# A two-layer hybrid network on one Trainium2 core: causal masks on the later keys alone, and a reciprocal in four pieces

## The chip, the cores and the metric

The kernel runs on one core of one Trainium2 chip. A core has a matrix engine (TensorE, PE in the profile, with its weight loads as PEld), a vector engine (VectorE, DVE), an engine for activations (ScalarE, ACT), a general one (GpSimd, POOL), and queues that issue DMAs (SyncE, SP, and others). Each engine works through its own instructions in order, and they wait for one another by semaphores. [...]

The metric is the device time of one execution in microseconds (us).

## The reference

The input is a batch of 32 sequences of 256 tokens with 128 features. Eight blocks are added to it one after the other, each behind a layer norm: a two-way state-space block, a mixture of experts, a recurrence, the same mixture again, then a windowed attention, a sparse mixture of experts, a causal attention with rotary positions, and a second sparse mixture. The change touches the two attentions. What they have in common, and where they differ:

```python
# the causal attention (the second one): 16 heads of 8 features
scores = jnp.einsum('bhqd,bhkd->bhqk', Q, K) / jnp.sqrt(jnp.float32(D_K))
causal = jnp.tril(jnp.ones((s, s), dtype=bool))
scores = jnp.where(causal[None, None], scores, -jnp.inf)
attn = jax.nn.softmax(scores, axis=-1)
out = jnp.einsum('bhqk,bhkd->bhqd', attn, V)

# the windowed attention (the first one): a query sees the up to 128 keys before it
allowed = (dist > 0) & (dist <= w) & (k_gpos[:, None, :] >= 0)
```

The softmax needs a maximum over each query's allowed keys, the exponentials, and a division by their sum.

## The kernel before

The features lie on the 128 partitions, and the tokens along the free dimension, in 16 chunks of 512 tokens (two sequences). A stage runs over the chunks as a software pipeline: `pipeline(chunk, 16, newest=True)` starts a chunk every 16 steps of the one before, so that two to three chunks are interleaved, and the order of the instructions on each engine follows from where the generators yield. The stages are the state-space block (up to about 2300 us in the profile), the first layer's mixtures and recurrence, the first attention (`l1_attn_a`, about 3370 to 4480 us) with the routing of its sparse mixture (`send`), the experts' blocks, the second attention (`l1_attn_b`, about 4970 to 6020 us) with the collection of what came before (`fetch`) and another routing, and again the experts' blocks.

Both attentions call `attend`. Its first pass only finds the maxima. For each of the two sequences (b), a first group of four PSUM banks takes the scores of the first 128 queries; then, for each half x of the heads, four banks take those of the last 128 queries against all 256 keys (two heads side by side in a bank, `j`, each with 256 keys, `k`). In each bank a bf16 matmul of an identity with a mask table writes 0 or -1e30 (`add_mask`, L918, which opens the accumulation), and a matmul of queries and keys adds the scores (L955 for the first queries, L978 for the second). VectorE takes the maximum over the keys (L964 and L982). The banks come from one pool with five buffers (tag `st`).

The second pass transposes the maxima, folds them into the queries (L1001 to L1004), and computes scores with the keys on the partitions: later keys with later queries (L1020), earlier keys with all queries (L1038). They go into banks of the same pool. ScalarE takes the exponential (L1029 and L1042), GpSimd sets the disallowed ones to zero (L922), and PE weighs the values with them (`weigh`, L1056), the sums of the exponentials coming along as a ninth row of each head. At the end of a chunk the sums are spread over the features of their heads (`dps`, L1093), VectorE takes the reciprocal of that 128x512 bank (L1095), the weighed values are packed (`ops`, L1099), and their product (L1100) is the attention's result. The output projection follows (L1643 in the second attention).

`masks.second` is what the mask matmul of the last 128 queries writes. For the windowed attention it lets a query at position q + 128 see the keys from q on to q + 127, and for the causal one (`k <= q1`) those up to q + 128. In the causal case every key of the first 128 is allowed.

Of the kernel before, what the change touches and what calls it, by code (L numbers as in the profile page):

```python
# [22 lines left out]
P = 128  # L23
B, L = 32, 256
# [170 lines left out]
def shape_constants():  # L195

    c = Packed()
    c.add("ident", np.eye(P, dtype=np.float32))
    c.add("center", np.eye(P, dtype=np.float32) - np.float32(1.0 / P))
    c.add("mean", np.full((P, 1), 1.0 / P, np.float32))  # L200
    c.add("mhalf", np.full((P, 8), -0.5, np.float32))
    c.add("states", (np.arange(P)[:, None] // 4 == np.arange(32)[None]).astype(np.float32))
    c1 = Packed()
    c1.add("rev", np.tile(np.arange(E, 0, -1, dtype=np.float32), (P, 4)))
    feat = np.arange(P)

    par = (feat[:, None] // 16) % 2 == np.arange(2)[None]
    c1.add("par", par.astype(np.float32))
    c1.add("ninth", (feat[:, None] % 16 == HD).astype(np.float32))
    for x in range(2):  # L210
        pk, dn = np.zeros((2, 8, 16, H, HD), np.float32)
        for h in range(8):
            pk[h, :HD, 8 * x + h, :] = np.eye(HD)
            dn[h, HD, 8 * x + h, :] = 1.0
        c1.add(f"pack{x}", pk.reshape(P, P))
        c1.add(f"den{x}", dn.reshape(P, P))
    c1.add("earlier", (np.arange(P)[:, None] < np.arange(P)[None]).astype(np.float32))
    c1.add("ones", np.ones((P, P), np.float32))
    c1.add("region", np.tile(np.arange(E, dtype=np.float32) * ROWS, (P, 1)))
    c1.add("filled", np.arange(0, NT, BLK, dtype=np.float32)[None])  # L220
    c1.add("upto", (np.arange(E)[None] <= np.arange(E)[:, None]).astype(np.float32).reshape(1, -1))
    c1.add("block", np.arange(NBLK, dtype=np.float32)[None])


    tok = np.arange(P)[:, None, None] + P * np.arange(4)[None, :, None]
    c1.add("home", (1.0 + 2 * tok + np.arange(2)[None, None]).reshape(P, 8))
    row = np.arange(P)[:, None, None] + BLK * np.arange(NBLK)[None, :, None] + P * np.arange(BLK // P)[None, None]
    c1.add("nowhere", (1.0 + 2 * NT + row).reshape(P, NBLK * BLK // P))
    c1.add("lheads", (np.arange(32)[:, None] // HD == np.arange(LH)[None]).astype(np.float32))

    rv = np.zeros((P, 2, 32), np.float32)
    for pr in range(2):
        for j in range(2):
            h = 2 * pr + j
            rv[j * NLAT : (j + 1) * NLAT, pr, h * HD : (h + 1) * HD] = 1.0
    c1.add("rvmask", rv)
    half = HD // 2
    inv = np.float32(10000.0) ** (-np.arange(half, dtype=np.float32) * np.float32(2.0) / np.float32(HD))
    ang = (np.arange(L, dtype=np.float32)[:, None] * inv[None]).astype(np.float32)
    at = (feat % HD) // 2  # L240
    used = (feat % 16 < HD)[:, None]
    cos = np.cos(ang)[:, at].T * used
    sin = np.sin(ang)[:, at].T * np.where(feat % 2 == 0, -1.0, 1.0)[:, None] * used
    c1.add("cosq", cos * SCALE)
    c1.add("sinq", sin * SCALE)
    c1.add("cosk", cos)
    c1.add("sink", sin)

    q = np.arange(P)[:, None]
    k = np.arange(L)[None]  # L250

    def add_mask(allowed, reps):
        return np.tile(np.where(allowed, 0.0, NEG), (1, reps))

    q1 = q + P
    first = (k < q)[:, :P]
    window = (k < q1) & (k >= q1 - P) & (k >= 1)
    lat = np.arange(NLAT)[None]
    masks = np.concatenate(
        [  # L260
            np.eye(P),
            add_mask(first, 4),
            add_mask(window, 2),
            add_mask((k <= q)[:, :P], 4),
            add_mask(lat < q // 4, LH),
            add_mask(lat < q1 // 4, LH),
            add_mask(k <= q1, 2),
        ],
        axis=1,
    ).astype(ml_dtypes.bfloat16)  # L270
    return c, c1, masks
# [3 lines left out]
def hybrid_kernel(ctx: ExitStack, tc, x_d, out_d, d, packs):  # L275
    nc = tc.nc
# [365 lines left out]
    mask_t = late.tile([P, d["masks"].shape[1]], BF16, name="mask_t")  # L642
# [271 lines left out]
    def rows(r):  # L914
        return slice(32 * r, 32 * r + 32)

    def add_mask(o, m):
        nc.tensor.matmul(o, identb, m, start=True, stop=False, skip_group_check=True)  # L918
# [14 lines left out]
    def attend(pools, qT, kT, kb, values, nms, masks, out):  # L933
# [5 lines left out]
        m_q0, m_q1 = masks.first, masks.second  # L939

        def banks():
            return [ps.tile([P, CH], F32, tag="st", name="st", bufs=5) for r in range(T)]
# [3 lines left out]
        for b in range(2):  # L946
            q0, q1 = slice(b * L, b * L + P), slice(b * L + P, (b + 1) * L)
            cut = slice(b * L, (b + 1) * L)
            n0, n1 = (t.rearrange("p (x h f) -> p x h f", x=2, h=8)[:, :, :, HD] for t in nms[b])
            s0 = banks()  # L950
            for o in s0:
                add_mask(o, m_q0)
            for x in range(2):
                for r, o in enumerate(s0):
                    nc.tensor.matmul(  # L955
                        o[:, x * L : (x + 1) * L],
                        qT[x][rows(r), q0],
                        kb[x][rows(r), :, q0],
                        start=False,
                        stop=True,  # L960
                        skip_group_check=True,
                    )
            for r, o in enumerate(s0):
                nc.vector.tensor_reduce(  # L964
                    n0[:, :, 2 * r : 2 * r + 2],
                    o.rearrange("p (x j k) -> p x j k", x=2, j=2),
                    AX.X,
                    ALU.max,
                    negate=True,
                )  # L970
            yield
            yield
            for x in range(2):
                s1 = banks()
                for o in s1:
                    add_mask(o, m_q1)
                for r, o in enumerate(s1):
                    nc.tensor.matmul(  # L978
                        o, qT[x][rows(r), q1], kb[x][rows(r), :, cut], start=False, stop=True, skip_group_check=True
                    )  # L980
                for r, o in enumerate(s1):
                    nc.vector.tensor_reduce(  # L982
                        n1[:, x, 2 * r : 2 * r + 2],
                        o.rearrange("p (j k) -> p j k", j=2),
                        AX.X,
                        ALU.max,
                        negate=True,
                    )
                yield
                yield  # L990
            if masks.window:

                nc.gpsimd.memset(nms[b][0][0:1, :], 0.0)
# [97 lines left out]
        dps = ps.tile([P, CH], F32, tag="m", name="dps")  # L1091
        for x in range(2):
            nc.tensor.matmul(dps, K(f"den{x}"), avs[x], start=(x == 0), stop=(x == 1))  # L1093
        rden = p2.tile([P, CH], F32, tag="rden", name="rden", bufs=1)
        nc.vector.reciprocal(rden, dps)  # L1095
        yield
        ops = ps.tile([P, CH], F32, tag="m", name="ops")
        for x in range(2):
# [39 lines left out]
    mo = P  # L1138
    m_first, m_window, m_causal, m_lat = (mask_t[:, mo + n * 512 : mo + (n + 1) * 512] for n in range(4))
    masks_a = Masks(m_first, m_window, True, 0)  # L1140
    masks_b = Masks(m_causal, mask_t[:, mo + 4 * 512 : mo + 5 * 512], False, 1)

# [275 lines left out]
    def l1_attn_a(send):  # L1420
        with ExitStack() as ph:
# [117 lines left out]
            def chunk(c):  # L1539
# [27 lines left out]
                for k, _ in enumerate(attend((p2, p3, ps), qT, kT, kb, values, nms, masks_a, local)):  # L1567
                    if k > 15:
                        next(side, None)
                    yield  # L1570
# [30 lines left out]
    def l1_attn_b(fetch, send):  # L1601
        with ExitStack() as ph:
# [6 lines left out]
            def chunk(c):  # L1609
# [25 lines left out]
                def values(b):  # L1635
                    project_values(ps, xin[:, b * L : (b + 1) * L], W("Wv"), None, vbs[b])
                    return vbs[b]

                yield from attend(
                    (p2, p3, ps), *([rot[n, y] for y in range(2)] for n in "qk"), kb, values, nms, masks_b, o  # L1640
                )
# [54 lines left out]
```

## Time and profile before

| | |
|---|---|
| median of 3 runs | 6514.0 us (6503.61 to 6520.93) |
| the profiled execution's own time | 6514.91 us |
| its span, first to last instruction | 6513.1 us |
| granted TensorE clock, mean over the span | 0.885 |
| TensorE busy | 5594.1 us (86%) |
| VectorE busy | 4202.2 us (65%) |
| ScalarE busy | 2688.5 us (41%) |
| GpSimd busy | 3325.7 us (51%) |
| mask matmuls (L918) | 768, of 0.379 us each in the median |
| reciprocals of the denominators (L1095) | 32, of 3.358 us each |

A busy share is a mean over stages with different limits. In a row of the timeline the first number is the start in us, the second the length of a run of like instructions (the last number behind x says how many), and a bracket gives how long the engine stood idle before it and what ended that. Successive matmuls overlap, so the pace of a run is the distance of its starts and not the length of one. The granted clock is the share of full speed at which TensorE ran.

### The profile page before, as it was taken

How to read it: one execution, taken by the hardware profiler on the slowest of the kernel's cores; microseconds unless marked ns; L12 is line 12 of the kernel's file. 1: busy time of each engine (PE TensorE's matmuls, PEld its weight loads, DVE VectorE, ACT ScalarE, POOL GpSimd, SP SyncE). 2: the span in 40 equal slices, each digit the busy share in tenths (PEclk: the TensorE clock that was granted, in tenths of full speed). 3: DMA queues.
4: the chain of work that ended last, by engine and by line, in shares of the span. 5: the costliest groups of instructions: out<-in, count | busy, mean ns of one | idle time of the engine just before them, and what ended most of it. 6: DMA issues, size and time to landing. Idle time of an engine off the chain costs nothing. (4 is left out here: it accounts for less than half of the span.)

```text
span 6513.1 us, 73037 instructions
## 1 busy us (share of the span) xinstructions
PE 5594.1 (86%) x25538; PEld 2738.9 (42%) x25538; DVE 4202.2 (65%) x6974; ACT 2688.5 (41%) x4391; POOL 3325.7 (51%) x3074
## 2 busy tenths in 40 slices
PE   6777777777777789999999899897998999998897
PEld 2111111111111146686544444443885444444786
DVE  5888888888888855304555555554665666664565
ACT  4555555555555435434433434433221332333221
POOL 4777777777777746304544444443332333333232
PEclk8888888888888789859999999997998999998898
DMA  3223223223223283000000000001552000000555
GB/s 149 110 92 123 104 91 118 110 95 120 104 92 119 77 331 138 1 1 1 1 1 4 9 9 8 10 9 45 188 188 67 14 17 17 17 14 11 168 186 189
DMA packets 190416, 512.20 MB, mean 79 GB/s; under 512 B 22176, under 2 KB 75168, under 8 KB 164960
## 3 DMA queue, kind: packets, MB, share of 16 engines
q1 hardware_dynamic: 172192, 468.14, 20.0%
q0 software_dynamic: 17280, 35.69, 1.6%
q8 instruction: 202, 3.31, 0.2%
q10 hardware_dynamic: 576, 3.71, 0.1%
q14 instruction: 166, 1.36, 0.1%
HBM read 360.06 MB, written 147.38 MB: 78 GB/s over the span
## 5 line engine op out<-in xcount | busy, mean ns | idle before, releaser
L598 POOL TENSOR_TENSOR dBu<-widedu,bcB 128x512 f32<-128x512 f32 x1024 | 1326.4, 1310 | 464.2 <-DVE h L607 340.3
L561 PE MATMUL yps<-pr,cst_t 128*32 128x512 f32 x2048 | 936.9, 731 | 492.2 <-DVE pr L609 214.7
L607 DVE TENSOR_TENSOR_SCAN h<-dA,dBu 128x512 f32<-128x512 f32 x768 | 941.1, 1225 | 68.9 <-POOL dBu L598 12.3
L922 POOL TENSOR_SCALAR_AFFINE_SELECT e<-e 128x2048 f32<-128x2048 f32 (+1 forms) x256 | 342.5, 1350 | 617.0 <-ACT e L1029 397.6
L561 PEld LDWEIGHTS yps<-pr,cst_t 128*32 128x32 f32 x2048 | 116.1, 117 | 1201.8 <-DVE pr L609 406.1
L594 ACT ACTIVATE dA<-widedelta,Af 128x510 f32<-128x510 f32 x512 | 348.9, 688 | 563.0 <-DVE h L607 440.4
L1392 POOL DMA_INDIRECT rows_out<-y,goes x284 | 271.8, 957 | 559.1 <-DVE y L1390 481.7
L982 DVE TENSOR_REDUCE nm<-st 128x2 f32<-128x512 f32 x512 | 324.1, 684 | 291.5 <-PE st L978 291.5
L594 ACT ACTIVATE dA<-widedelta,Ab 128x510 f32<-128x510 f32 x512 | 347.4, 687 | 394.5 <-DVE h L607 294.2
L1167 ACT ACTIVATE s<-s 128x512 f32<-128x512 f32 x284 | 178.9, 630 | 577.0 <-DVE s L1166 347.2
L315 POOL TENSOR_TENSOR rstd<-var,cst_t 128x4 f32<-128x4 f32 x128 | 130.0, 1015 | 521.5 <-DVE var L313 519.8
L767 POOL TENSOR_TENSOR comb<-comb,ye 128x512 f32<-128x512 f32 x224 | 284.8, 1275 | 181.8 <-DVE ye L766 75.2
L607 DVE TENSOR_TENSOR_SCAN hs<-dA,dBu 128x512 f32<-128x512 f32 x256 | 310.6, 1213 | 95.4 <-POOL dBu L598 95.4
L1042 ACT ACTIVATE e<-st 128x512 f32<-128x512 f32 x512 | 271.7, 598 | 175.3 <-PE st L1038 174.4
L556 POOL TENSOR_TENSOR pr<-hs,bcC 128x512 f32<-128x512 f32 x256 | 338.5, 1322 | 1.4 <-DVE hs L607 1.4
L609 DVE TENSOR_TENSOR pr<-h,bcC 128x1024 f32<-128x1024 f32 x256 | 309.8, 1210 | 8.0 <-PE yps L561 0.9
L1281 POOL DMA_INDIRECT rows_in<-xt,slot x256 | 254.0, 992 | 119.4 <-issue 99.4
L1373 PE MATMUL g_ps<-xb,gu 128*128 128x256 f32 x1136 | 302.6, 389 | 3.6 <-ACT xb L1356 2.3
L1168 DVE TENSOR_TENSOR hh<-s,u_ps 128x512 f32<-128x512 f32 x284 | 195.4, 688 | 170.2 <-ACT s L1167 164.2
L1382 PE MATMUL yps<-dn,hh 128*128 128x128 f32 x2272 | 291.0, 275 | 5.1 <-DVE hh L1168 5.1
L1373 PE MATMUL u_ps<-xb,gu 128*128 128x256 f32 x1136 | 293.3, 381 | 0.0
L1382 PEld LDWEIGHTS yps<-dn,hh 128*128 128x128 f32 x2272 | 282.6, 192 | 14.1 <-DVE hh L1168 6.6
(348 smaller groups left out, 11083.1 us busy)
## 6 DMA issues: line engine op xcount, KB each, us to landing
gu<-in_gu SPq DMA_DIRECT2D x142, 512.0 KB, 3.8
rows_in<-zero SPq DMA_DIRECT2D x60, 1170.0 KB, 18.8
widedelta<-delta_d SPq DMA_DIRECT2D x64, 1024.0 KB, 6.8
widedu<-du_d SPq DMA_DIRECT2D x64, 1024.0 KB, 5.0
dn<-in_dn SPq DMA_DIRECT2D x142, 256.0 KB, 4.0
bcB<-xdbl_d SPq DMA_DIRECT2D x32, 1024.0 KB, 7.6
bcC<-xdbl_d SPq DMA_DIRECT2D x32, 1024.0 KB, 7.3
xr<-rows_in SPq DMA_DIRECT2D x142, 130.0 KB, 3.9
```

What stands on the lines that cost most here:

```text
L556: nc.gpsimd.tensor_mul(pr, hs, bc["C"][:, g, :])
L561: nc.tensor.matmul(yps[32 * k : 32 * k + 32, :], K("states"), pr, start=False, stop=(g == 3), skip_group_check=True, tile_position=(0, 32 ...
L594: nc.scalar.activation(two(dA)[:, :, 1:L], two(steps)[:, :, 1:L], AF.Exp, scale=A[s][:, at : at + 1])
L598: nc.gpsimd.tensor_mul(dBu, duw[:, k, :], bc["B"][:, g, :])
L607: nc.vector.tensor_tensor_scan(*views, 0.0, ALU.mult, ALU.add)
L609: nc.vector.tensor_mul(pr2, h2, bc["C"][:, g, :].unsqueeze(1).to_broadcast([P, 2, CH]))
L767: nc.gpsimd.tensor_add(comb, comb, ye)
L922: nc.gpsimd.affine_select(e, e, [[0, n], [sign, P]], ALU.is_gt, 0.0, base=base, channel_multiplier=-sign)
L982: nc.vector.tensor_reduce(n1[:, x, 2 * r : 2 * r + 2], o.rearrange("p (j k) -> p j k", j=2), AX.X, ALU.max, negate=True,)
L1373: nc.tensor.matmul(o[:, j, :], gu[:, at : at + P], xb, start=True, stop=True)
L1382: nc.tensor.matmul(yps[:, t, :], hh[:, k, t * P : (t + 1) * P], dn[:, k, :], start=(k == 0), stop=(k == FF // P - 1),)
L1392: i = nc.gpsimd.indirect_dma_start(rows_out[:, :], bass.IndirectOffsetOnAxis(ap=goes[:, t : t + 1], axis=0), y[:, t, :], None)
```

## The change

There are two edits. In the causal attention, the mask matmuls of the second queries write only the keys 128 to 255 of each of the two heads of a bank: an output of two runs of 128 columns. The keys before, all allowed, are left unwritten by the mask, and the score matmul, which does not open an accumulation, writes them. The table for it is the first 256 columns of the mask of the first queries, which has the same triangle. The old table is dropped, so that the mask table becomes 512 columns narrower. The windowed attention keeps its masks. The other edit is in both attentions: the reciprocal of the 128x512 denominators becomes four of 128x128.

```diff
             add_mask(lat < q1 // 4, LH),
-            add_mask(k <= q1, 2),
         ],
...
                 for o in s1:
-                    add_mask(o, m_q1)
+                    if masks.window:
+                        add_mask(o, m_q1)
+                    else:
+
+                        add_mask(o.rearrange("p (j k) -> p j k", j=2)[:, :, P:L], m_q1.rearrange("p (j k) -> p j k", j=2))
...
         rden = p2.tile([P, CH], F32, tag="rden", name="rden", bufs=1)
-        nc.vector.reciprocal(rden, dps)
+
+        for t in range(4):
+            nc.vector.reciprocal(rden[:, t * P : (t + 1) * P], dps[:, t * P : (t + 1) * P])
...
-    masks_b = Masks(m_causal, mask_t[:, mo + 4 * 512 : mo + 5 * 512], False, 1)
+    masks_b = Masks(m_causal, m_causal[:, 0:L], False, 1)
```

## The prediction

> **What bounds the kernel now.** I read the page first, for which engine is full and where, then the busy time of the two attention stages, then one chunk of the second attention in order of time, then the sources of the two lines that the change touches.
>
> ```profile
> span 6513.1 us, 73037 instructions
> ...
> PE 5594.1 (86%) x25538; PEld 2738.9 (42%) x25538; DVE 4202.2 (65%) x6974; ACT 2688.5 (41%) x4391; POOL 3325.7 (51%) x3074
> ```
>
> TensorE (PE) is the fullest engine, but that is a mean over stages. Both edits act between 3370 and 6020 us only (L918 runs there, and L1095 does). The busy time of those two stages:
>
> ```profile
> 4970.00:6020.00 1050.00, 979.60 (x5955) 456.94 (x5953) 663.59 (x1368) 330.69 (x567) 327.09 (x308) 0.94 0.05 15
> 3370.00:4480.00 1110.00, 1005.26 (x6332) 462.20 (x6331) 631.45 (x1392) 441.02 (x771) 457.31 (x645) 0.93 0.02 8
> ```
>
> Columns are the stage, its length, then busy time of PE, weight loads, VectorE (DVE), ScalarE (ACT), GpSimd (POOL), then granted clock and DMA. PE is busy for 93% and 91%, DVE for 63% and 57%. PE sets the pace; DVE matters where PE waits for it. The mask writes on PE, from the timeline of one chunk (start, length, engine, line):
>
> ```profile
> 5411.35 1.02 PE L918 MATMUL st<-mask_t 128*128 128x512 bf16 x4
> 5412.30 1.14 PE L978 MATMUL st<-kb,rotq 32*128 32x512 f32 x8
> ...
> 5434.16 0.39 PE L918 MATMUL st<-mask_t 128*128 128x512 bf16 x1
> 5435.46 1.35 PE L918 MATMUL st<-mask_t 128*128 128x512 bf16 x3 [0.91 <-ACT e L1042]
> 5436.74 1.14 PE L978 MATMUL st<-kb,rotq 32*128 32x512 f32 x8
> ```
>
> The first group is free: four masks stream, and the scores (L978) follow 0.95 us after the first. The second is paced: its masks wait for ScalarE to give up score banks, and only the last one's length counts. The other line:
>
> ```profile
> L1095 DVE RECIPROCAL rden<-dps x32: 3358/3358/3359, 3467.2 to 6012.4; 128x512 f32<-128x512 f32 x32
> ```
>
> ```profile
> L1507 DVE RECIPROCAL den<-den x32: 193/200/204, 3431.4 to 4458.7; 128x8 f32<-128x8 f32 x32
> ```
>
> ```profile
> 3814.47 3.36 DVE L1095 RECIPROCAL rden<-dps 128x512 f32<-128x512 f32 x1 [1.01 <-PE dps L1093]
> ...
> 3817.75 2.42 DVE L964 TENSOR_REDUCE nm<-st 128x4 f32<-128x512 f32 x4
> 3817.89 0.30 PEld L1099 LDWEIGHTS ops<-avs,cst_t 128*128 128x128 f32 x2 [2.09 <-DVE rden L1095]
> ```
>
> The reciprocal costs 3.36 us and PE stands behind it. The waits of PE in the first attention say how often (total us, times, longest), and those of its weight loads in the second:
>
> ```profile
> PE ops L1099 <- DVE rden L1095: 16.6, 14, 1.2
> ```
>
> ```profile
> PEld av L1056 <- POOL e L922: 29.3, 17, 5.6
> ...
> PEld ops L1643 <- DVE o L1100: 13.4, 16, 4.2
> ```
>
> **The change part by part.** The engines' instruction order stays as it was: ACT, POOL and SP issue the same sequence, DVE has 96 instructions more (3 for each of 32 chunks), and PE has the same count, with two places in the first chunk of the second attention where a mask and a score matmul change places. So nothing is moved past anything; what changes is the length of 256 mask matmuls and of 32 reciprocals.
>
> *Mask table.* 512 of 2688 columns go (128 KB of one 672 KB load, issued at 2305 us and landed 12.6 us later). First use is at 3365 us, so it is worth nothing; if something did wait on it, a fifth of 12.6 us.
>
> *Masks of the second queries, second attention alone.* 16 chunks, 2 sequences, 2 halves: 64 groups of 4. A 512-column mask lasts 0.379 us alone, and four take 1.03 us, so the pace is (1.03 - 0.379)/3 = 0.217 us. Half the columns: 0.109 us. Each mask still loads the 128x128 identity, at 98 ns (L918, weight load), just under that. The nearest row with a fresh full weight load per short matmul is the transposes of L1213: four in 0.65 us at 0.273 each, a pace of 0.126. So a mask gains 0.09 to 0.108 us; I take 0.105, a group 0.42. Going through all 63 groups that the timeline separates (two of the first chunk run together): 38 are free at full clock, 7 free in a stretch of half clock (pace 0.43, gain 0.84), 18 paced by ACT's 0.49 us or DVE's 0.60 us per bank. A paced group can gain 0.1 at its last mask, but what follows it in the chunk is a wait of PE for POOL (L1056 <- L922 above), which eats some; I take 0.05. Sum: 38 x 0.42 + 7 x 0.84 + 18 x 0.05 = 22.8 us. It stays on the path because what follows a free group hangs on it: the row maxima (L982) wait for L978 (127 us of DVE idle over 63 waits), the next scores wait for L982's banks, ACT's exponentials for those.
>
> [...] The new output is two runs of 128 columns with a gap. [...] No row here writes PSUM with a gap. The nearest are the score matmuls of L955, which read two runs of 128: 16 of them take 1.15 us, exactly as L1020's 16 that write the same bank width. That is a read, so it bounds nothing on the write side. [...]
>
> *Reciprocal in four.* From the two rows, an element costs (3358 - 200)/504 = 6.27 ns. The next instruction starts 3.27 or 3.28 us after the reciprocal (3814.47 to 3817.75), 512 elements are 3.21, so 0.06 to 0.07 us is paid per instruction; four pieces pay it three times more: 0.18 to 0.21, and I take 0.21. No piece waits: all read the one finished bank. [...] Behind the pieces on DVE stand the row maxima L964 and the product L1100. Who waits: in the first attention PE at L1099, whose bank the reciprocal holds (14 chunks); in the second PE at L1643, behind L1100 (16 chunks). The last two chunks of the first attention have slack. 30 x 0.21 = 6.3 us. Nothing is gained by the split: nothing on DVE gets between the pieces, and the bank is freed only by the last.
>
> *Sum.* -22.8 + 6.3 = -16.5 us on the profiled execution. That ran 6514.9 us (span 6513.1 and 1.8 around it), 0.9 above the median of the runs shown. 6514.9 - 16.5 = 6498. Neither edit has a large unknown of its own; the clock has. By the granted clock in the trace, about 13.6 us of every two chunks of the second attention run at half clock, in steps of 3.4 us, and by the starts of L1095 the chunks alternate between 64.0 and 65.7 us: their sum, 129.7, is 38 such steps. A chunk shortened by 1 us can fall otherwise on these steps. One step more or less in every second chunk is up to 8 x 1.7 = 14 us. That is the width I give it, both ways, though half of it is likelier.
>
> **The rivals.**
> *A: the gain comes whole or larger.* The half-clock steps fall better, or the reciprocal's tail is hidden behind PE work (the first attention fills part of the wait with L1442). Then -23 to -30: about 6488. For it: 7 free groups lie in half clock. Against: PE's idle time stays and PE's work falls, which is no reason for a better clock.
> *B: the gain is eaten.* The chunk stays locked to 38 steps, or the shortened masks meet a full set of 5 score banks, and the free groups become paced ones. Then the masks give 0 to 8 and the reciprocals take 6.3: 6507 to 6521. For it: 18 groups are paced already. Against: in the free group shown, ACT (0.49 us a bank, from 5409.67) has given back the third bank at 5411.25, and the fourth mask would need it at 5411.35 + 3 x 0.11 = 5411.7.
> *C, slower: the gapped write.* Place: the 45 free groups, 180 masks. If a column into the gapped output takes four cycles in place of one, 256 of them take 0.43 us where 512 took 0.217: 180 x 0.213 = 38 us, and 6.3 for the reciprocals: 6559. It decides from a pace of 0.29 us on: 180 x (0.29 - 0.217) + 6.3 = 19.5. [...]
> *That the change does not do what it says* is excluded by the order of instructions: 256 masks are 128x2x128, 128 reciprocals are 128x128.
>
> **How the numbers follow.** Forecast 0.60 (6490 to 6508), A 0.18, B 0.12, C 0.10. 0.3% is about what a measurement of this kernel can tell from no change: 19.5 us, so faster means below 6494.5. All of A and about a third of the forecast lie there: 0.18 + 0.18 = 0.36. C is the slower case: 0.10, and B ends within the bound. Within 0.3%: 0.54. The range takes the forecast, B, and the nearer half of A: 6482 to 6522, leaving out C and the far end of A.
>
> **What would show it.** Right: L918 keeps 512 matmuls of 512 columns in the two stages and has 256 new ones whose fours start 0.11 to 0.13 us apart in free groups, L978 following 0.52 to 0.55 us after the first; L1095 has 128 pieces of about 0.95 us, with 3.46 to 3.50 us from the first to the L964 behind it; the distance of reciprocals from chunk to chunk falls by about 1 us in the second attention and grows by about 0.2 in the first. Wrong: fours paced at 0.2 us or more (C), more half-clock time in the second attention than its 146 us (B), or a pace between the pieces far from 0.87 us.

## The result and the profile after

| | before | after |
|---|---|---|
| median us (lowest to highest) of six runs | 6505.3 (6494.6 to 6520.9) | 6478.6 (6471.8 to 6483.6) |
| ratio after to before, 95% interval | | 0.9958 [0.9948, 0.9969] |
| the profiled execution's own time | 6514.9 | 6483.6 |
| mean granted TensorE clock in it | 0.885 | 0.882 |

The change is faster by 27 us (20 to 34), where 16.5 were forecast. The three runs of before that came beside those of after took 6494.6 to 6506.9 us, the first three 6503.6 to 6520.9, so that the median of all six lies 8.7 us below the 6514.0 of the first table. Against the three that came beside it alone, with a median of 6502.9, the change gains 24 us.

In the changed kernel the lines have moved: the mask is L917, the scores of the second queries L981 and their maxima L985, the maxima of the first queries L963, the reciprocal L1100, the matmuls behind it L1104 and the product L1105. The head of its page:

```profile
span 6481.8 us, 73077 instructions
...
PE 5558.2 (86%) x25466; PEld 2746.5 (42%) x25538; DVE 4206.2 (65%) x7070; ACT 2686.6 (41%) x4391; POOL 3326.3 (51%) x3074
```

TensorE is busy for 36 us less; 72 of its matmuls (25466 of 25538) have no record in this trace, and a small part of the 36 may be theirs. VectorE has its 96 instructions more and is busy for 4 us more. Both attention stages, the first one first (stage, length, busy PE, weight loads, DVE, ACT, POOL, then granted clock, DMA share, GB/s):

```profile
3376.00:4474.00 1098.00, 986.36 (x6305) 460.34 (x6361) 632.36 (x1438) 441.52 (x772) 457.50 (x646) 0.94 0.02 8
4962.00:5989.00 1027.00, 951.23 (x5939) 464.77 (x5951) 667.32 (x1416) 330.55 (x567) 327.21 (x308) 0.92 0.05 15
```

The second attention ran at 0.94 before and runs at 0.92 now: it is shorter although its clock is lower. Measured from its first projection to the start of its last packing matmul (L1099 before, L1104 after), the first attention went from 1115.8 to 1103.1 us and the second from 1046.7 to 1024.9.

The masks, from the timeline of PE in the second attention, first a paced group and then a free one:

```profile
5284.71 0.28 PE L917 MATMUL st<-mask_t 128*128 128x256 bf16 x1
5286.00 1.35 PE L917 MATMUL st<-mask_t 128*128 128x256 bf16 x3 [1.01 <-ACT e L1045]
...
5392.81 0.60 PE L917 MATMUL st<-mask_t 128*128 128x256 bf16 x4
5393.34 1.14 PE L981 MATMUL st<-kb,rotq 32*128 32x512 f32 x8
```

In the free group four masks take 0.60 us; one lasts 0.28, so the pace is (0.60 - 0.28)/3 = 0.11 us, and the scores follow 0.53 us after the first, where it was 0.95. In the paced group three take 1.35 us as before: ScalarE gives up a bank every 0.5 us at either width. Now the reciprocal, as a source and in one chunk of the first attention:

```profile
L1100 DVE RECIPROCAL rden<-dps x128: 893/895/959, 3474.0 to 5985.4; 128x128 f32<-128x128 f32 x128
```

```profile
3821.61 3.39 DVE L1100 RECIPROCAL rden<-dps 128x128 f32<-128x128 f32 x4 [1.01 <-PE dps L1096]
...
3824.93 1.22 DVE L963 TENSOR_REDUCE nm<-st 128x4 f32<-128x512 f32 x2
3825.12 0.30 PEld L1104 LDWEIGHTS ops<-avs,cst_t 128*128 128x128 f32 x2 [2.19 <-issue]
3825.15 1.10 PE L1104 MATMUL ops<-avs,cst_t 128*128 128x512 f32 x2 [1.31 <-DVE rden L1100]
```

Four pieces take 3.39 us where one instruction took 3.36, and the next VectorE instruction starts 3.32 us after the first piece, where it was 3.28. PE's matmul behind it starts 3.54 us after the first piece; before, it was 3.42 in the same chunk:

```profile
3817.89 1.55 PE L1099 MATMUL ops<-avs,cst_t 128*128 128x512 f32 x3 [1.18 <-DVE rden L1095]
```

PE waits there as often as before, in 14 chunks, and a little longer each time:

```profile
PE ops L1104 <- DVE rden L1100: 18.3, 14, 1.3
```

It was 16.6 in all: (18.3 - 16.6)/14 = 0.12 us each. By the starts it is 0.12 to 0.13 us in each of these 14 chunks.

### The profile page after: what moved, and what is told of

The parts are those of the page before. It is cut to its first block, busy times and chain, and to the rows that moved or that the text cites. A ratio compares the mean times of both kernels' runs of the same rounds, so it can differ in the third digit from the quotient of the medians.

```text
span 6481.8 us, 73077 instructions
## 1 busy us (share of the span) xinstructions
PE 5558.2 (86%) x25466; PEld 2746.5 (42%) x25538; DVE 4206.2 (65%) x7070; ACT 2686.6 (41%) x4391; POOL 3326.3 (51%) x3074
## 5 line engine op out<-in xcount | busy, mean ns | idle before, releaser
L985 DVE TENSOR_REDUCE nm<-st 128x2 f32<-128x512 f32 x512 | 324.2, 684 | 266.4 <-PE st L981 264.7
```

What stands on the lines that cost most here:

```text
L985: nc.vector.tensor_reduce(n1[:, x, 2 * r : 2 * r + 2], o.rearrange("p (j k) -> p j k", j=2), AX.X, ALU.max, negate=True,)
```

## The experiments

The theory was that the masks make the gain and the split costs little or nothing. Against it stood: the split is worth something by itself; the gap in the output costs a part of the gain; the clock takes part of the gain back. The experiments ran on four chips, whose medians for the kernel before differ (6505 to 6542 us). So every row is a ratio to the kernel before on its own chip, and only rows of one chip are compared in us.

| experiment | chip | before, us | this, us | ratio [95%] | us [95%] |
|---|---|---|---|---|---|
| e1, split alone | I | 6542.1 | 6539.5 | 0.9996 [0.9983, 1.0009] | -3 [-11, +6] |
| e2, masks alone | I | 6542.1 | 6529.0 | 0.9980 [0.9970, 0.9991] | -13 [-20, -6] |
| e3, masks without a gap | I | 6542.1 | 6529.4 | 0.9989 [0.9975, 1.0003] | -7 [-16, +2] |
| e4, reciprocal in 16 | I | 6542.1 | 6547.3 | 1.0016 [1.0007, 1.0025] | +10 [+5, +16] |
| e5, both | II | 6505.4 | 6483.3 | 0.9969 [0.9957, 0.9981] | -20 [-28, -12] |
| e6, kernel before | II | 6505.4 | 6500.2 | 0.9994 [0.9986, 1.0003] | -4 [-9, +2] |
| e7, masks twice | II | 6505.4 | 6542.9 | 1.0053 [1.0039, 1.0067] | +34 [+25, +44] |
| e8, none of these masks | II | 6505.4 | 6471.9 | 0.9954 [0.9940, 0.9967] | -30 [-39, -21] |
| e9, no mask matmul at all | III | 6534.6 | 6508.1 | 0.9955 [0.9939, 0.9972] | -29 [-40, -18] |
| e10, masks alone | III | 6534.6 | 6517.1 | 0.9970 [0.9960, 0.9981] | -20 [-26, -12] |
| e11, split alone | III | 6534.6 | 6528.6 | 0.9990 [0.9982, 0.9999] | -7 [-12, -1] |
| e12, both | IV | 6533.4 | 6508.6 | 0.9966 [0.9953, 0.9980] | -22 [-31, -13] |
| e13, masks alone | IV | 6533.4 | 6518.1 | 0.9976 [0.9966, 0.9985] | -16 [-22, -10] |
| e14, split in the first attention | IV | 6533.4 | 6530.3 | 1.0001 [0.9989, 1.0013] | +1 [-7, +8] |
| e15, reciprocal lengthened | IV | 6533.4 | 6547.0 | 1.0020 [1.0008, 1.0031] | +13 [+5, +20] |

The last column is the ratio less one times the median of before. The ratio is not always the quotient of the two medians (e3 has -7 us by it and -13 by the medians, e4 +10 and +5); the intervals belong to the ratio. e6, the unchanged kernel against itself, shows what a row is good to.

**The two parts, each alone (e1, e2, and again e10, e11, e13).**

```diff
# e1, e11
-        nc.vector.reciprocal(rden, dps)
+        for t in range(4):
+            nc.vector.reciprocal(rden[:, t * (CH // 4) : (t + 1) * (CH // 4)], dps[:, t * (CH // 4) : (t + 1) * (CH // 4)])
# e2, e10, e13: the change's mask edits, with the reciprocal whole
```

> The reciprocal in four pieces alone, masks as before. The sum of the prediction: 30 x 0.21 = 6.3 us slower than the kernel before. The clock theory (the four pieces shift the first attention so that fewer of its half-clock steps fall on busy stretches, as the profile after shows: 121 us of half clock there against 150): about 8 us faster, -14 in the first attention and +3 in the second. If the split costs nothing at all: no change.

> The masks on later keys alone, reciprocal whole. The sum of the prediction: 22.8 us faster than before, first attention unchanged. The clock theory: the first attention keeps its 150 us of half clock and its 1110 us, and the second is 20 to 26 us shorter, so 20 to 26 faster, and the rest of the 27 us of both edits comes from the split. If the gain of both edits were the masks' alone: 27 to 33 us faster.

> The masks on later keys alone, once more, beside the split alone and the kernel before on one chip. Corrected sum: -22.8 for the masks, the whole effect of both edits: 20 to 25 faster. If the masks are worth only the 0.2% of the first such run: 10 to 15 faster.

> The split alone, once more. Corrected price, four pieces 0.03 us longer than one: 30 x 0.03 = 1 us, no change within the measurement. The prediction's 6.3 us slower would be 0.1%. A gain of the split by itself: 5 us faster or more, its interval below 1.

> The masks alone: 13 and 19 us faster than before in the two earlier runs; 13 to 23 faster here. The prediction's term: 22.8.

The masks alone give -13, -20 and -16 us; the counted -22.8 lies 3 us outside the first interval, just outside the third and inside the second. The split alone gives -3 and -7: the +6.3 of the prediction lies outside both intervals, just so in e1 and by 7 us in e11. That is the step that fell.

**The gap in the output (e3).** One run of 256 columns in place of two of 128, with the reciprocal whole. It masks other keys, so what is masked is not the reference's; the work is of the same shape otherwise.

```diff
-                        add_mask(o.rearrange("p (j k) -> p j k", j=2)[:, :, P:L], ...)
+                        add_mask(o[:, 0:L], m_q1)
```

> As the masks alone, but each of these masks writes one run of 256 columns in place of two runs of 128 with a gap (so it falls on the first head's 256 keys, and the masking is another one). If the gap costs nothing: the same time as the masks alone within 5 us, and the same pace of 0.106 to 0.109 us in free groups. If a gapped output costs anything: faster than the masks alone by 180 times the difference in pace.

A free group from its timeline:

```profile
5401.23 0.60 PE L917 MATMUL st<-mask_t 128*128 128x256 bf16 x4
5401.76 1.14 PE L981 MATMUL st<-kb,rotq 32*128 32x512 f32 x8
```

0.60 and 0.53 us, to the last digit those of the gapped write. The price of the gap is nil at this size, and rival C had no ground.

**More pieces (e4).** The split with 16 in place of 4.

> The reciprocal in sixteen pieces alone. A price of 0.07 us for every further instruction: 15 x 0.07 = 1.05 us per chunk, 30 x 1.05 = 32 us slower than before. If the clock of the first attention decides, the time need not follow the number of pieces: between -10 and +32, with a half-clock time in the two attentions that differs from before's 150 and 135 us by more than 10 us.

From its timeline of VectorE:

```profile
5484.25 3.53 DVE L1096 RECIPROCAL rden<-dps 128x32 f32<-128x32 f32 x16 [0.64 <-PE dps L1093]
5487.70 2.42 DVE L964 TENSOR_REDUCE nm<-st 128x4 f32<-128x512 f32 x4
```

Sixteen take 3.53 us where one takes 3.36: 0.17/15 = 0.011 us for each piece more. The next instruction starts 3.45 us after the first, 0.17 later than with one. So fifteen more instructions cost VectorE less than the prediction charged for three (0.21). For PE it is more: in the first attention the matmul behind the reciprocal starts 0.46 us later than with one piece in nine of the 14 chunks. In four others it starts 0.9 us earlier, for in this kernel TensorE's own instructions lie in another order in some 28 places. So the measured +10 us [+5, +16] is not a price of the pieces alone.

**The whole change again, and the kernel before against itself (e5, e6, e12).**

> The change whole, once more. The masks alone gave 0.2% and the split nothing on the chip of the last runs. If both edits add up: -22.8 for the masks as counted in the prediction, +1 for the split (its four pieces measured 3.39 us against 3.36), so -22, less what the clock gives back. Clock theory (less TensorE work in a 3.4 us step means more steps at half clock in the second attention): -12 to -20, with 170 to 215 us of half clock there against 126 to 140 with the whole masks. If the first result of -27 is the masks' alone: -24 to -30.

> The kernel before against itself: no change. It gives the spread of the measurement, a profile of the kernel before on this chip, and the half-clock time of its attentions: near 140 us in the second one if that belongs to the masks' length, anywhere up to 215 if it is chance.

> Both edits, beside the masks alone on one chip, so that the split's share is the difference. Counted on the traces: the split delays L1099 in the first attention by 0.13 us a chunk and the next VectorE instruction by 0.03, 14 x 0.13 + 16 x 0.03 = 2.3 us, so both edits 2 us slower than the masks alone. The prediction's term: 6.3 us slower than them. Clock theory (the split keeps the first attention off its half-clock steps): 5 to 10 us faster than them.

-20 and -22 us, with -27 in the first measurement. Their intervals share -20 to -28. On chip IV the whole change is better than the masks alone by 0.001 of the time, 6.5 us, with an uncertainty of about 11: the split may give a little, and this doesn't show it.

**A scale of mask work (e7, e8, e9).** In the second attention alone, the masks of the second queries twice, or not at all (their maxima then run over all 256 keys); in e9 no mask matmul in either first pass (all maxima over all 256 keys). The reciprocal is whole in all three.

```diff
# e7, behind add_mask(o, m_q1)
+                    if not masks.window:
+                        add_mask(o, m_q1)
# e8
-                    add_mask(o, m_q1)
+                    if masks.window:
+                        add_mask(o, m_q1)
...
-                        o, qT[x][rows(r), q1], kb[x][rows(r), :, cut], start=False, stop=True, skip_group_check=True
+                        o, qT[x][rows(r), q1], kb[x][rows(r), :, cut], start=not masks.window, stop=True, skip_group_check=True
# e9: both loops of add_mask removed, start=True in L955 and L978
```

> Each mask matmul of the second queries in the second attention is issued twice, 512 columns each, with the same result. Without a response of the clock: 45 free groups x 4 x 0.217 = 39, and 18 x 0.2 = 4 for the paced ones, 43 us slower. Clock theory: less half-clock time in the second attention than with single masks (below 126 us), so only 20 to 35 us slower.

> No masks for the second queries in the second attention: the scores open the accumulation themselves. What is left out: the maxima are then taken over all keys and not over the allowed ones alone, an upper bound that softmax may subtract as well; GpSimd still zeroes the disallowed exponentials. Without a response of the clock: 38 x 0.87 + 7 x 1.74 + 18 x 0.2 = 49 us faster than before, about twice the masks on later keys. Clock theory: over 200 us of half clock in the second attention, and 20 to 35 us faster. Rival: the score banks bind (scores have to wait for them where masks waited), then not faster than the masks on later keys.

> No mask matmuls at all in the first pass of both attentions. What is left out: the maxima are taken over all keys of a bank, an upper bound of the allowed ones' that softmax may subtract as well; GpSimd still zeroes the disallowed exponentials. Dropping the second queries' masks of one attention gave -33 (0.46%) for 256 of the 768 masks; the other 512 stream or are paced in the same way in half of the stretches, so -33 x 3 = -100 if the response is even, -60 to -75 if the score banks and the clock's half-speed steps take their part as they did there (49 counted, 33 measured).

The second attention on chip II, from the windows of e7, e6, e5 and e8, one kernel a fence (the granted clock is the third value from the end). Each is a single execution, for e7 the slowest of its runs and for e5 and e8 the fastest of theirs:

```profile
4980.00:6050.00 1070.00, 1003.96 (x6122) 473.15 (x6166) 654.47 (x1350) 330.75 (x567) 324.61 (x306) 0.95 0.05 14
```

```profile
4980.00:6005.00 1025.00, 957.24 (x5859) 450.53 (x5899) 651.66 (x1357) 330.06 (x566) 323.35 (x304) 0.94 0.05 15
```

```profile
4965.00:5975.00 1010.00, 935.97 (x5887) 459.81 (x5898) 654.32 (x1393) 330.61 (x567) 324.75 (x306) 0.92 0.05 15
```

```profile
4970.00:5970.00 1000.00, 924.93 (x5643) 450.49 (x5653) 656.80 (x1348) 330.05 (x567) 325.79 (x306) 0.90 0.05 15
```

With 1024, 512, 256 and 0 mask columns a bank the clock goes 0.95, 0.94, 0.92, 0.90. The steps of the clock in the trace add up to 109, 135, 167 and 202 us at half clock in this stage (first kernel before: 138, first kernel after: 174). The stage's whole length, by the same reckoning as above, is 1086, 1041, 1025 and 1012.5 us.

Twice the masks cost 45 us, which is what the pace gives: 38 x 4 x 0.217 + 7 x 4 x 0.434 = 45. None of them should then give as much, 38 x 0.95 + 7 x 1.9 = 49 by the times from mask to scores, and gives 28; half gives 16 here and 22 between the first two profiles, where 22.8 was counted. With less TensorE work came more time at half clock, 135 us, then 167 and 202. In the kernel before a mask's pace at half clock was 0.43 us, at full clock 0.217, so 202 - 135 = 67 us more at half clock can cost at most half of that, 33 us, were TensorE the limit all along; 49 - 28 = 21 are missing. TensorE was busy in nearly all of that time (131 of the 135 us, 194 of the 202), so the clock is the likely cause; but the order of VectorE's instructions also differs in some 27 places in e8, so that it is not shown for all of the 21.

The other chips agree on the clock. On I, III and IV the five kernels with whole masks have 127 to 156 us at half clock in the second attention (e1, e4, e11, e14, e15), the five with halved ones 191 to 222 (e2, e3, e10, e12, e13). On chip IV, whose traces have a record of nearly every matmul, TensorE's busy time in the second attention hardly changes: 977 us in e14 and in e15, 975 and 981 in e12 and e13. The 84 to 96 us more at half clock are enough to take back what it was spared. These stages are shorter all the same, 1052 and 1060 us for 1070 and 1063, since TensorE stands idle for 77 to 79 us in place of 86 to 93. Between the first two profiles it was the other way: TensorE was busy for 27 us less (980.5 and 953.3) and idle for 5 us more.

e9 goes on that way. It has no mask matmul left, and its second attention ran as follows:

```profile
4973.00:6030.00 1057.00, 937.41 (x5495) 454.67 (x5494) 631.95 (x1344) 332.23 (x571) 323.66 (x305) 0.85 0.05 14
```

A clock of 0.85, 327 us at half clock. On its chip the masks alone (e10) had 212, and a second attention of 1061.8 us; e9, with still less work, needs 1073.2. Two things besides the clock are mixed in here: VectorE waits for 42 us at its product with the rotary table, where e10 waits for 29 (see below), and its instructions lie in another order in some 170 places. What e9 gained it gained in the first attention, 1077.7 us for e10's 1121.7; but e10's profiled execution was the slowest of its 15, and with that code this stage takes 1102 us as well (e13). In all it is no better than e8 by its ratio. e8 has the lowest ratio of all, 0.9954 [0.9940, 0.9967], on a chip where the whole change has 0.9969 [0.9957, 0.9981]; the intervals overlap.

**Where the split acts (e14, e15).** The first attention alone, and a reciprocal made longer by a second one over its first 16 columns.

```diff
# e14
+        pieces = 4 if masks.window else 1
+        for t in range(pieces):
+            part = slice(t * CH // pieces, (t + 1) * CH // pieces)
+            nc.vector.reciprocal(rden[:, part], dps[:, part])
# e15
         nc.vector.reciprocal(rden, dps)
+        nc.vector.reciprocal(rden[:, 0:16], dps[:, 0:16])
```

> The reciprocal in four pieces in the first attention alone. Local count: 14 x 0.13 = 2 us slower. Clock theory: 5 to 10 us faster, the first attention's half-clock time below 110 us.

> The reciprocal whole, and a second one over its first 16 columns behind it (the same result): about 0.12 us more VectorE time at the same place, with no split. Local count: 30 x 0.12 = 4 us slower. If any delay of this size at this place moves the first attention off its half-clock steps: as with the split, 3 to 8 us faster. If the split itself does it: not faster.

e14 is nil within 8 us: no gain of the split in the first attention is seen, and none near the 13 us by which the first two profiles differ there. e15 does not do what it was meant to. From its timeline:

```profile
3825.63 3.36 DVE L1095 RECIPROCAL rden<-dps 128x512 f32<-128x512 f32 x1 [0.96 <-PE dps L1093]
3828.91 0.63 DVE L964 TENSOR_REDUCE nm<-st 128x4 f32<-128x512 f32 x1
3829.45 0.24 DVE L1096 RECIPROCAL rden<-dps 128x16 f32<-128x16 f32 x1
...
3829.75 1.98 PE L1100 MATMUL ops<-avs,cst_t 128*128 128x512 f32 x4 [1.89 <-DVE rden L1096]
```

A row maximum went between the two, so PE started 4.12 us after the reciprocal in place of 3.42: 0.70 us later, not 0.12. At 0.70 it is 14 x 0.70 = 10 us for the first attention alone and 30 x 0.70 = 21 for all; +13 [+5, +20] lies between. It shows that a delay of this size at this place costs time, and says nothing on one of the split's size.

## Why the prediction fell short

**Right.** The masks' pace: 0.11 us in free groups, L981 0.53 us behind the first (0.52 to 0.55 was said); the paced groups kept ScalarE's pace of 0.5 us. That the masks carry most of the gain: three runs of them alone, -13 to -20 us. The sum of the mask groups comes to 22.7 and not 22.8, which changes nothing. That a write in two runs keeps the pace of one run: the 22.8 rests on that, and no row of the kernel before shows it, which has no such write; it was my estimate. e3 shows it, four masks in 0.60 us and the scores 0.53 us behind the first with the gap and without. Shorter runs are not tried. Right too was that VectorE's order stays, with nothing between the pieces.

**The step that failed: "30 x 0.21 = 6.3 us" for the split.** The prediction took the 0.06 us between one reciprocal and a row maximum for a price of each instruction. Between two reciprocals it is 0.011 us (e4), so four pieces add 0.03 to 0.04 on VectorE; the matmul behind them starts 0.12 later in the chunk shown and in the mean of 14 waits. The prediction had one delay for both engines, and they have different ones. Counted again: 14 x 0.12 in the first attention and, in the second, where VectorE's next instruction is what counts, 16 x 0.04, 2.3 us in all. The runs of the split alone lie lower still, -3 [-11, +6] and -7 [-12, -1] us: that the split does not cost 6.3 is shown, and why it does not even cost 2.3 is not. The 3.46 to 3.50 us that I named as a sign from the first piece to L963 came out as 3.32.

**The size.** With that term the sum is -22.8 + 2.3 = -20.5 us, inside the intervals of all three measurements of the whole change (-27, -20, -22), just so in the first. That it fits is luck in part: alone, the masks gave less than their term (13 to 20 us) and the split cost less than its own, and the two errors about cancel. The forecast's -16.5 is inside the second and third and outside the first. The predicted time was 19.4 us above the measured median. 9.6 of these are the base, the second term that failed, since the execution that was profiled first ran 6514.9 us and the six runs have 6505.3; 4.0 are the split; the other 5.8 lie within the interval of the ratio. The range was missed by 3.4 us, so the base alone would have been enough for that, and the split's 4.0 just. The prediction compared its execution with the median of three runs and found it 0.9 above; that median itself stood too high, and the spread of its three runs, 17 us, should have been carried into the range's lower end.

**The clock, half right.** It was the unknown that I named. I gave it 14 us both ways and said that falling TensorE work was no reason for a better clock. Here it came with a worse one: more than 146 us of half clock in the second attention was my sign for rival B (138 by the limits of the stage used here), and 174 came. Yet B did not follow, for the stage was 22 us shorter all the same. The sign was badly chosen: more time at half clock does not say whether the stage gets longer. The masks alone fall short of -22.8 by 3 to 10 us in their three medians, which is what a give-back would look like; the clock is the likely taker where the masks are gone (e8), and on chip IV the traces show it for halved masks too, though there a shorter idle time hides part of it.

**The chunks.** I said about 1 us less from chunk to chunk in the second attention and 0.2 more in the first. The second gave 21.8/16 = 1.4 less. The first gave 0.8 less, where the split alone could only cost. Its half clock was 147 us before and 119 after in these two profiles. The first attentions of e1, e2, e10, e11, e13 and e14, which have the old or the split reciprocal and the same masks, took between 1098.8 and 1121.7 us, and those of e2, e10 and e13, with one and the same code, 1121.5, 1121.7 and 1102.1. So a difference of 13 us between two profiles there is within what one kernel does by itself, and is not put down to the split. Over all traces with these masks the stage takes 1098 to 1103 us in the six with the reciprocal split there and 1101 to 1122 in the eight with it whole. But five of those six executions were faster than the median of their kernel, and five of the other eight were slower, so this is no proof of a gain either.

**The rivals.** A named the size (-23 to -30 against -27 in the first measurement) and not the reason: the half-clock steps did not fall better where the masks are, and the two later measurements (-20 and -22) lie below its size. B's size is out: in e10 and e13 the masks give more than 8 us. A trace of its reason is there, for PE's masks wait for ScalarE 27 times in the second attention in place of 14, for 17.3 us in place of 12.9. C is out by the pace in e3 and in the changed kernel, 0.11 us a mask in both; the fourfold time per column that it supposed is in no run.

**Still open.** Whether the split gives something: e1, e11 and the difference of e12 and e13 all point to a gain of 3 to 7 us, e14 does not, and no row of the trace shows where it would come from. Open too is what makes the chips differ. On chips I, III and IV every profile has a wait of VectorE in the second attention, at its product with the rotary table, whose releaser the profile doesn't know. From the waits of VectorE in e11:

```profile
DVE nm L982 <- PE st L978: 120.5, 62, 5.0
DVE rotk L1625 <- remote: 50.6, 13, 4.5
```

With the masks whole it is 50 to 52 us in 13 waits (e1, e4, e11, e14, e15), with them halved 21 to 29 in 6 to 8 (e2, e10, e12, e13) and 37 in 10 (e3). It does not simply follow the masks' length, for with none it is 42 in 11 (e9). In the first two profiles and on chip II it is absent. The second attention takes 1070 us in e1 and e14 against 1041 in e6, about the 28 to 37 us by which the medians of the chips lie apart. On chip IV TensorE's idle time in that stage fell by 7 to 16 us with the masks halved while its busy time hardly changed, so the masks' gain on these chips may well lie in this wait; what VectorE waits for there was not tried.

## What to carry to other kernels

Cut matmul columns where the first consumer hangs on the last column and the banks are free, and count those groups one by one: the free ones went at the pace that was counted (0.11 us a mask), those paced by another engine took as long as before (1.35 us for three). Charge an instruction that is cut in pieces with the distance between two of its own kind, not with the distance to the next kind of instruction (0.011 us here, and not 0.06), and read the start of the engine that waits for the last piece by itself. On chip IV nearly all of the work taken off TensorE came back as time at half clock (84 to 96 us more of it, TensorE busy for 975 and 981 us after 977): read the granted clock and TensorE's idle time beside every gain. And where the runs of a kernel spread as widely as the gain that is forecast, start from their median and carry their spread into the range.

## What the runs showed of the hardware

- A reciprocal from PSUM costs 6.4 ns a column, (3.358 - 0.895)/384, and splitting it 0.011 us a piece on VectorE (3.36, 3.39 and 3.53 us in 1, 4 and 16). A matmul that waits for it starts 0.12 to 0.13 us later behind four pieces (14 chunks of the first attention).
- A bf16 matmul that writes PSUM in two runs of 128 fp32 columns goes at the pace of one run of 256: 0.11 us.
- With TensorE busy for 89 to 94% of the second attention, it still ran there at half clock for 109 to 327 us of 1010 to 1090: 127 to 156 us with whole masks, 167 to 222 with halved ones, 202 and 327 with none. On chip II it was the more, the less mask work there was (109, 135, 167 and 202 us). In the traces of the kernel before and of the changed one the clock is full or half, in stretches of 3.41 us or a multiple of that; no run shows what decides which.
- Executions of one kernel on one chip lie 0.2 to 0.8% apart from the fastest to the slowest, and the lower the mean granted clock of an execution, the longer it takes (correlations of -0.74 to -0.85 for the kernel before on four chips, -0.54 to -0.98 for the others).
